# A second stream of early forward transforms in a two-layer image kernel

## The chip, the cores and the metric

The kernel runs on one core of a Trainium2 chip. A core has five engines that each work through their own instruction list in order: PE (TensorE, matrix products into PSUM), ACT (ScalarE, activation functions and copies), DVE (VectorE), POOL (GpSimd) and SP (SyncE, which issues nearly all DMAs here). They meet only through semaphores. The metric is the time of one execution on the device in microseconds (us), smaller being better.

## The reference

Everything is float32. The input `x` has the shape (4, 128, 128, 128): four batch entries, 128 channels, images of 128x128. Two layers follow one another.

The first layer takes the 16384 pixels of a batch entry as one sequence of tokens. Each token passes a small MLP, a projection to two halves of 256, a causal convolution of four taps, and then a state space scan with 256 channels and 16 states:

```
h = h * dA + d_t * B_t * u_t          # per channel and state, along the 16384 tokens
y = sum over states of h * C_t
out = (y + u * D) * silu(z) @ out_proj_w.T
x1 = silu(group_norm(out)) + x
```

The second layer works on whole images of `x1`. It transforms, multiplies with four learned filters that are mixed by four weights, and transforms back:

```
weights = softmax(mean(relu(agg_w @ group_norm(x1))) @ wg_w.T + wg_b)   # 4 weights per batch entry
xf      = rfft2(x1)
out     = irfft2(xf * xf * sum_f weights[f] * filt_f) + 0.5 * x1
```

(The reference transforms back and forth between the filter and the product; the kernel uses that this changes little more than single columns of the spectrum, and multiplies directly.) The mixture weights of a batch entry need the whole of its `x1`, but the forward transform `rfft2` of an image needs only that image.

## The kernel before, in words

There are two Python functions, `block0` and `block1`, that emit one after the other the instructions of the two layers. In both the order on every engine is written out by hand (a manual schedule); the tile framework adds semaphores and buffer waits.

**`block0`.** The tokens of each batch entry are cut into 32 chunks of 512, so there are 128 chunks `k`. A chunk has 32 scans of 128 partitions by 512 tokens, in 16 *slots* (`NP = 16`) of two scans each. The list `todo[slot, phase]` holds closures, and the loop at the end of `block0` walks over absolute slots `16*k + s`, and within a slot over the phases `turn, sums, pe, exps, late, act, pool, dbu, early, gate, scans, dve, end`. What a closure emits takes that place in the list of whatever engines it uses. The parts that matter here:

- `exps` (L393, ACT) makes the decay factors `da` for the scans of the next slots, `scans` (L412, DVE) does two scans per slot and, for half of them, the product with `C` (L414). The tiles `da1`, `da2` and `da3` have one buffer each, so ACT can't run far ahead of DVE.
- `dbu_turn` (L383, PE) turns the input term of one scan in two slots into PSUM; `sums` (L433, PE) adds up states into `y`.
- `pre(k)` computes chunk `k`'s inputs during chunk `k-1`: `cv_mm(0)` and `cv_mm(1)` (L234, PE) stand in slots 0 and 1, `silu_act` (L239) and `z_silu` (L242) in slot 2, `xd_mm` (L247) in slot 3, transposes `pt_dut` (L293) in slots 8 and 11 with their ACT copies `bt` (L304) up to slot 14. `turn_bank` is a single PSUM buffer (tag `pt`) that `xd_mm`, the transposes and a few others share; `psum` hands out two buffers (tag `pp`).
- `finish` turns the raw output of a batch entry `b` into `x1` while the next entry is being scanned. In the first 18 chunks of an entry it normalises the previous one (`norm_act` L633 on ACT in slot 2, `norm_dve` L637 and `norm_stats` L641 on DVE in slot 3, two pieces per chunk); I call these *norm chunks*. From chunk 18 on it runs the aggregation (`agg`), one piece per chunk, the last four of them in the `pt` bank at slot 15.
- `spectrum(b, c0, n)` computes the forward transform of `n` images of batch entry `b` early, in `block0`, and stores it in DRAM (`spec_b`). A *unit* is eight channels of one batch entry; it is done as three sub-units of 3, 3 and 2 images, one sub-unit per chunk. Its five steps have fixed slots: `load` (4, SP), `over_h` (12, PE), `evict` (12 end, ACT copy `fs`), `over_w` (13, PE), `store` (13 end, ACT copy `fq` and a DMA). It takes both matmul results in `pp`. Batch entries 0 and 1 are eligible (`EARLY = 2`). From chunk 52 to chunk 126 this makes 25 units: all 16 of entry 0, and channels 0 to 71 of entry 1.

**`block1`.** The second layer is 64 units in the list `units`. A unit takes three *steps* (3, 3, 2 images); step `t` belongs to unit `t // 3`. Each step emits `over_h` (L851, PE), `evict`, `residual`, `conjugates` (L860, DVE), `products` (DVE), `over_w` (L874, L875, PE), `back_h` (L913, L914, PE), `back_w` (L925, PE), and each unit four scaled filters `term` (L822, ACT), three `mix` additions (L828, POOL) and two `sums` (L899, L900, POOL). For an early unit `over_h`, `conjugates` and the matmuls of `over_w` are left out; its spectrum `sx` is loaded (L815) instead. The units of entry 3 come late, because entry 3 must first be normalised and aggregated, which `finish` does in the first 36 units. `load(n + 1)` is emitted at step 0 of unit `n`, behind the filter loads `load_filter` (L805, four DMAs of 520 KB for a group of eight channels, `KEEP = 4` buffers). All of them are on SP's queue.

Of the kernel before, what the change touches and what calls it, by code (L numbers as in the profile page):

```python
# [26 lines left out]
F32 = mybir.dt.float32  # L27
# [6 lines left out]
P = 128  # L34
T = 512
DG = 32
SQ = 4
NP = 16
CC = 8
EARLY = 2  # L40
KEEP = 4
LAG = 7
EPS = 1e-5
# [3 lines left out]
def kernel(ctx: ExitStack, tc: tile.TileContext, a: dict, out: bass.AP):  # L47
    nc = tc.nc
    x = a["x"]
    B, C, H, W = x.shape  # L50
    L = H * W
    NCH = L // T
# [9 lines left out]
    WF = W // 2 + 1  # L62
# [3 lines left out]
    dpool = ctx.enter_context(tc.tile_pool(name="dram", bufs=1, space=DRAM))  # L66
# [79 lines left out]
    xflat = x.rearrange("b c h w -> b c (h w)")  # L146

    stats, outs, spectra = {}, {}, set()
    spec = [dpool.tile([H, C, 2, WF], F32, tag=f"spec_{b}", name=f"spec_{b}") for b in range(EARLY)]
    shared = SimpleNamespace(**{k: v for k, v in locals().items() if k not in ("ctx", "tc")})  # L150
    block0(tc, shared)
    block1(tc, shared)
# [2 lines left out]
def block0(tc, s):  # L155
    nc, B, NCH, NH, NS, NG, ND, R, NX, KC, HALO, C, L, NF, DI = (
        s.nc, s.B, s.NCH, s.NH, s.NS, s.NG, s.ND, s.R, s.NX, s.KC, s.HALO, s.C, s.L, s.NF, s.DI,
    )
    NT = T // P
    with ExitStack() as ctx:  # L160
        def pool(name, bufs, **kw):
            return ctx.enter_context(tc.tile_pool(name=name, bufs=bufs, **kw))
# [7 lines left out]
        psp = pool("psp", 2, space=PSUM)  # L170
        psy = pool("psy", 1, space=PSUM)
        pst = pool("pst", 1, space=PSUM)
        psd = pool("psd", 1, space=PSUM)

        def psum(n):
            return psp.tile([P, T], F32, tag="pp", name=f"pp_{n}")

        def turn_bank(n):
            return pst.tile([P, T], F32, tag="pt", name=f"pt_{n}")

        st = {}
        stats, outs = s.stats, s.outs
# [282 lines left out]
                (50, "dve", done),  # L465
            ]

        def spectrum(b, c0, n):

            g = {}  # L470

            def load():
                g["x"] = p1.tile([s.H, 3, s.W], F32, tag="fx", name=f"fx_{b}_{c0}")
                nc.sync.dma_start(out=g["x"][:, 0:n], in_=s.x1[b][c0 : c0 + n].rearrange("c h w -> h c w"))

            def over_h():
                g["pa"] = psp.tile([s.W, 3, 2 * s.WF], F32, tag="pp", name=f"pp_fa_{b}_{c0}")
                for q in range(n):
                    nc.tensor.matmul(g["pa"][:, q], g["x"][:, q], s.fh, start=True, stop=True)

            def evict():
                g["sa"] = p1.tile([s.W, 3, 2 * s.WF], F32, tag="fs", name=f"fs_{b}_{c0}")
                nc.scalar.copy(g["sa"][:, 0:n], g["pa"][:, 0:n])

            def over_w():
                half = s.H // 2
                g["px"] = psp.tile([s.H, 3, 2 * s.WF], F32, tag="pp", name=f"pp_fx_{b}_{c0}")
                for q in range(n):
                    re, im = g["sa"][:, q, 0 : s.WF], g["sa"][:, q, s.WF :]
                    for (data, a, b_), start in (((re, s.fwr, s.fwr), True), ((im, s.fwi, s.fwm), False)):  # L490
                        for at, w in ((0, a), (1, b_)):
                            o = g["px"][at * half : (at + 1) * half, q]
                            nc.tensor.matmul(o, data[:, at : at + half], w, start=start, stop=not start)

            def store():
                x = p1.tile([s.H, 3, 2, s.WF], F32, tag="fq", name=f"fq_{b}_{c0}")
                nc.scalar.copy(x[:, 0:n].rearrange("h c r k -> h c (r k)"), g["px"][:, 0:n])  # L497
                nc.sync.dma_start(out=s.spec[b][:, c0 : c0 + n], in_=x[:, 0:n])

            return [  # L500
                (4, "pe", load), (12, "pe", over_h), (12, "end", evict), (13, "pe", over_w), (13, "end", store),
            ]

        n_chunks = B * NCH
        todo = defaultdict(list)
# [19 lines left out]
        for b in range(B - 1):  # L525
            for at, phase, f in finish(s, io, b, NP + 7, norm, agg):
                todo[at + (b + 1) * NCH * NP, phase].append(f)
        chunk = NCH + NCH // 2 + 4
        for b in range(EARLY):
            for c0 in range(0, C, CC):  # L530
                chunk = max(chunk, (b + 1) * NCH + NCH // 2 + 4)
                if chunk + 3 > n_chunks:
                    break
                for at, n in ((0, 3), (3, 3), (6, 2)):
                    for slot, phase, f in spectrum(b, c0 + at, n):
                        todo[slot + chunk * NP, phase].append(f)
                    chunk += 1
                s.spectra.add((c0, b))
        for n in range(n_chunks * NP):
            if n % 2 == 0:  # L540
                todo[n - 3, "early"].append(partial(exps, n, (0,)))
# [7 lines left out]
        slots = [n for n, _ in todo]  # L549
# [172 lines left out]
def block1(tc, s):  # L722
# [7 lines left out]
    nc, B, C, H, W, WF, NF, NCH = s.nc, s.B, s.C, s.H, s.W, s.WF, s.NF, s.NCH  # L730
    HH = H // 2
    filt = s.a["filt_w"].rearrange("f c h w q -> h f c (w q)")
    with ExitStack() as ctx:
        def pool(name, bufs, **kw):
            return ctx.enter_context(tc.tile_pool(name=name, bufs=bufs, **kw))

        late = pool("late", 1)
# [30 lines left out]
        todo = defaultdict(list)  # L768
# [8 lines left out]
        rest = groups[len(wait) :]  # L777
        kept, late = wait[-KEEP + 1 :], wait[: -KEEP + 1]
        units = [(c0, b) for c0 in wait for b in (0, 2, 1)] + [(c0, B - 1) for c0 in kept]
        for n, c0 in enumerate(rest):  # L780
            units += [(c0, b) for b in (0, 2, 1, 3)]
            for c1 in late[n * len(late) // len(rest) : (n + 1) * len(late) // len(rest)]:
                units.append((c1, B - 1))
        N = len(units)
        u = [SimpleNamespace() for _ in units]

        spans = []
        for n, (c0, b) in enumerate(units):
            ft = next((x for x in spans if x.c0 == c0 and (n - x.last == 1 or (c0 in kept and b == B - 1))), None)
            if ft is None:  # L790
                ft = SimpleNamespace(c0=c0, first=n)
                spans.append(ft)
            ft.last = n
            u[n].ft = ft
        loads = defaultdict(list)
        for k, ft in enumerate(spans):
            at = max(ft.first - 4, min(k, 1))
            if k >= KEEP:
                at = max(at, spans[k - KEEP].last)
# [7 lines left out]
        def load(n):  # L807
            if n < N:
                c0, b = units[n]
                u[n].xt = p2.tile([H, CC, W], F32, tag="xt1", name=f"xt1_{n}", bufs=6)  # L810
                nc.sync.dma_start(out=u[n].xt, in_=s.x1[b][c0 : c0 + CC].rearrange("c h w -> h c w"))
                u[n].early = units[n] in s.spectra
                if u[n].early:
                    u[n].sx = p2.tile([H, CC, 2, WF], F32, tag="sx", name=f"sx_{n}", bufs=2)
                    nc.sync.dma_start(out=u[n].sx, in_=s.spec[b][:, c0 : c0 + CC])  # L815

        def term(n, f):

            if 0 <= n < N:
                tag, bufs = ("term", 3) if f else ("wb", 2)  # L820
                t = p2.tile([H, CC, 2 * WF], F32, tag=tag, name=f"{tag}_{n}_{f}", bufs=bufs)
                nc.scalar.activation(t, u[n].ft.t[:, f], AF.Copy, scale=s.wts[units[n][1]][0:H, f : f + 1])  # L822
                u[n].terms = [t] if f == 0 else u[n].terms + [t]

        def mix(n, f):
            if 0 <= n < N:
                wb = u[n].terms[0]
                nc.gpsimd.tensor_tensor(wb, wb, u[n].terms[f], ALU.add)  # L828
# [107 lines left out]

        with tc.manual_schedule():
            load(0)
            for t in range(3 * N + LAG + 3):
                n, i = divmod(t, 3)  # L940
                if i == 0:
                    for ft in loads[n]:
                        load_filter(ft)
                    load(n + 1)
                over_h(t)
                if t == 0:
                    for f in range(NF):
                        term(0, f)
                        if f:
                            mix(0, f)  # L950
                evict(t - LAG - 1)
                residual(t - LAG - 2)
                conjugates(t)
                products(t - 2)
                for f in todo[t, "add"]:
                    f()
                over_w(t - 1)
                back_h(t - LAG)
                back_w(t - LAG - 1)
                if i == 0:  # L960
                    if n:
                        term(n, 3)
                        mix(n, 2)
                    copies(n - 2)
                elif i == 1:
                    term(n + 1, 0)
                    term(n + 1, 1)
                    if n:
                        mix(n, 3)
                else:  # L970
                    term(n + 1, 2)
                    sums(n - 1)
                    mix(n + 1, 1)
                for phase in ("pe", "act", "dve", "end"):
                    for f in todo[t, phase]:
                        f()
# [79 lines left out]
```

## Time and profile before

| what | value |
|---|---|
| median of 3 runs | 7170.91 us (7170.88 to 7171.45) |
| the profiled execution's own time | 7175.45 us |
| its span | 7173.6 us |
| first scan of the first chunk, last chunk's last part | 48.7 us, about 6404 us |
| first and last store of the output | 6466.8 us, 7169.5 us |
| chunk without any finishing work (chunks 20 to 22) | 48.37 / 49.12 us in turn |
| norm chunk (40 to 42; 104 to 106) | 50.3 us |
| PE, DVE, ACT, POOL busy share of the span | 82%, 96%, 86%, 96% |
| TensorE clock granted, mean | 0.897 |

The profile comes from one execution. An engine's row counts the time in which it executes, not the time in which it issues DMAs or waits. In rows of a timeline the first number is the start in microseconds from the span's start and the second is the duration; a bracket behind it gives the idle time before, and what ended it. `L412` is line 412 of the kernel. A name such as `da<-rdelta,amat` says which tile an instruction writes and which it reads. Rows of matmuls count each float32 product as two instructions.

### The profile page before, as it was taken

How to read it: one execution, taken by the hardware profiler on the slowest of the kernel's cores; microseconds unless marked ns; L12 is line 12 of the kernel's file. 1: busy time of each engine (PE TensorE's matmuls, PEld its weight loads, DVE VectorE, ACT ScalarE, POOL GpSimd, SP SyncE). 2: the span in 40 equal slices, each digit the busy share in tenths (PEclk: the TensorE clock that was granted, in tenths of full speed). 3: DMA queues.
4: the chain of work that ended last, by engine and by line, in shares of the span. 5: the costliest groups of instructions: out<-in, count | busy, mean ns of one | idle time of the engine just before them, and what ended most of it. 6: DMA issues, size and time to landing. Idle time of an engine off the chain costs nothing.

```text
span 7173.6 us, 91384 instructions
## 1 busy us (share of the span) xinstructions
PE 5904.2 (82%) x26708; PEld 2626.8 (37%) x26708; DVE 6892.9 (96%) x7966; ACT 6143.9 (86%) x13658; POOL 6892.5 (96%) x3188
## 2 busy tenths in 40 slices
PE   6888888788787788888888788888887888867998
PEld 2333333233222233333333333333333333326888
DVE  6999999999999999999999999999999999989777
ACT  6888888888888888888888888898888888878876
POOL 6999999999999999999999999999999999988887
PEclk8888888888888889998989899999898899979999
DMA  5666666666777777777777777777777777769866
GB/s 139 160 160 152 163 159 151 165 159 165 191 176 192 179 171 176 172 184 175 189 196 186 188 176 175 178 177 184 189 191 194 177 179 177 172 164 306 236 185 162
DMA packets 905480, 1286.20 MB, mean 179 GB/s; under 512 B 81672, under 2 KB 356752, under 8 KB 904976
## 3 DMA queue, kind: packets, MB, share of 16 engines
q1 hardware_dynamic: 904832, 1280.09, 71.9%
q8 instruction: 210, 3.44, 0.2%
q14 instruction: 294, 2.41, 0.1%
q10 hardware_dynamic: 144, 0.26, 0.0%
HBM read 1023.45 MB, written 256.58 MB: 178 GB/s over the span
## 4 chain that ended last, share of the span: by engine, by line
DVE 41%; ACT 29%; issue 11%; PE 10%; DMA 5%; POOL 3%; SPq 1%; DVEq 0%; ACTq 0%; POOLq 0%
DVE da L412 20%; DVE h L412 12%; ACT da L393 12%; DVE hb L414 5%; ACT L393 3%; DMA rdelta<-dd 2%; ACT L275 2%; ACT delta L275 2%; ACT bt L304 2%; POOL hb L363 2%; DVE zs L443 1%; PE y L433 1%; POOL hb L419 1%; ACT L242 1%; DMA xt<-x 1%
## 5 line engine op out<-in xcount | busy, mean ns | idle before, releaser
L363 POOL TENSOR_TENSOR hb<-rdu,rB 128x1536 f32<-128x1536 f32 (+2 forms) x1536 | 3605.7, 2364 | 22.4 <-DMA rdelta<-dd 21.3
L393 ACT ACTIVATE da<-rdelta,amat 128x512 f32<-128x512 f32 x4096 | 2794.1, 700 | 138.3 <-DVE h L412 133.9
L419 POOL TENSOR_TENSOR hb<-h,rC 128x1024 f32<-128x1024 f32 (+1 forms) x1072 | 2435.0, 2274 | 88.8 <-DVE h L412 73.4
L412 DVE TENSOR_TENSOR_SCAN da<-da,st,hb 128x512 f32<-128x512 f32 x1976 | 2419.8, 1267 | 21.5 <-ACT da L393 14.3
L433 PE MATMUL y<-hb,sel 128*32 128x512 f32 x8192 | 1313.4, 717 | 2.9 <-POOL hb L419 2.7
L414 DVE TENSOR_TENSOR hb<-da,rC 128x512 f32<-128x512 f32 x2040 | 1296.1, 674 | 3.0
L412 DVE TENSOR_TENSOR_SCAN h<-da,st,b 128x512 f32<-128x512 f32 x992 | 1258.3, 1268 | 1.7 <-PE b L383 1.6
L412 DVE TENSOR_TENSOR_SCAN h<-da,st,hb 128x512 f32<-128x512 f32 x1000 | 1251.6, 1255 | 1.8 <-ACT da L393 1.8
L383 PE MATMUL b<-ident,bt 128*128 128x128 f32 x4096 | 748.4, 305 | 516.1 <-DVE h L412 390.6
L234 PE MATMUL pp_cv<-xm,wck 128*128 128x512 f32 x2048 | 1014.3, 640 | 1.6 <-ACT xm L217 0.8
L304 ACT ACTIVATE bt<-pt_dut,xdt 128x256 f32<-128x256 f32 x2048 | 839.4, 474 | 184.5 <-PE pt_dut L293 184.3
L383 PEld LDWEIGHTS b<-ident,bt 128*128 128x128 f32 x4096 | 531.3, 154 | 1017.1 <-DVE h L412 692.8
L415 ACT COPY st<-da 128x1 f32<-128x1 f32 x2040 | 273.1, 160 | 474.2 <-DVE hb L414 471.1
L234 PEld LDWEIGHTS pp_cv<-xm,wck 128*128 128x128 f32 x2048 | 395.9, 204 | 651.0 <-issue 422.1
L828 POOL TENSOR_TENSOR wb<-wb,term 128x1040 f32<-128x1040 f32 x192 | 461.0, 2401 | 70.8 <-ACT term L822 62.9
L293 PE MATMUL pt_dut<-ident,du 128*128 128x128 f32 x1024 | 232.4, 338 | 285.1 <-ACT xdt L286 174.9
L429 PE MATMUL y<-u,diag 128*128 128x512 f32 x512 | 303.0, 675 | 188.7 <-DVE zs L443 187.3
L293 PEld LDWEIGHTS pt_dut<-ident,du 128*128 128x128 f32 x1024 | 132.2, 162 | 604.8 <-POOL du L312 475.9
L393 ACT ACT_TABLE_LOAD x262 | 336.1, 1283 | 12.1 <-DMA rdelta<-dd 7.4
L312 POOL TENSOR_TENSOR du<-delta,u 128x512 f32<-128x512 f32 x256 | 318.8, 1267 | 25.8 <-ACT delta L275 25.8
L223 PE MATMUL pp_z<-xm,win 128*128 128x512 f32 x512 | 274.5, 634 | 51.8 <-ACT fq L497 46.2
L267 PE MATMUL pp_dt<-xd,wdt 8*128 8x512 f32 x512 | 284.8, 642 | 33.0 <-ACT pp_o L457 23.5
(160 smaller groups left out, 8139.8 us busy)
## 6 DMA issues: line engine op xcount, KB each, us to landing
rdelta<-dd SPq DMA_DIRECT2D x1024, 256.0 KB, 4.7
rdu<-dd SPq DMA_DIRECT2D x1024, 256.0 KB, 7.5
rC<-bc SPq DMA_DIRECT2D x512, 256.0 KB, 7.3
rB<-bc SPq DMA_DIRECT2D x512, 192.0 KB, 4.7
dd<-delta SPq DMA_DIRECT2D x256, 256.0 KB, 7.2
dd<-du SPq DMA_DIRECT2D x256, 256.0 KB, 5.7
ft<-in_filt_w SPq DMA_DIRECT2D x104, 520.0 KB, 7.0
ob<-o SPq DMA_DIRECT2D x128, 256.0 KB, 2.1
```

The lines of the kernel that those rows point to most:

```text
L234: nc.tensor.matmul(ps["cv", j], w, d["xm"][:, t : t + T], start=t == 0, stop=t == KC - 1)
L293: nc.tensor.transpose(ps["dut"][:, 2 * t + j, :], d["du"][:, j, at : at + P], s.ident)
L304: nc.scalar.activation(d["bt"][:, 2 * h + t, :, q, :], src, AF.Copy, scale=d["xdt"][:, 2 * h + t, R + q : R + q + 1])
L312: nc.gpsimd.tensor_tensor(du, d["delta"][:, j, :], d["u"][:, j, :], ALU.mult)
L363: nc.gpsimd.tensor_tensor(hb[:, p : p + n, :], d["du", j][:, m : m + n, :], d["B"][:, p - 1 : p - 1 + n, :], ALU.mult)
L383: nc.tensor.transpose(b[:, t * P : (t + 1) * P], src, s.ident)
L393: nc.scalar.activation(da, d["delta", j][:, m, :], AF.Exp, scale=s.amat[:, c : c + 1])
L412: nc.vector.tensor_tensor_scan(o, das[q], b, init, ALU.mult, ALU.add)
L414: nc.vector.tensor_tensor(hb[:, p + q, :], das[q], d["C"][:, p + q, :], ALU.mult)
L419: nc.gpsimd.tensor_tensor(hb[:, ps, :], h[:, q, :], d["C"][:, ps, :], ALU.mult)
L433: nc.tensor.matmul(y[m * DG : (m + 1) * DG, :], s.sel, d["hb", j, r][:, p, :], start=False, stop=r == NG - 1)
L828: nc.gpsimd.tensor_tensor(wb, wb, u[n].terms[f], ALU.add)
```

## The change

In `block0` a second stream of early units is added. The two streams are called `ways`: the old one with its slots and the `pp` buffers, and a new one with the slots `load` 13 (SP), `over_h` 15 (PE), `evict` 16 (ACT), `over_w` 17 (PE, which is slot 1 of the next chunk) and `store` 17 end, with the `pt` bank as its home. Entries 0, 1 and 2 are eligible now, and within an entry the last channels come first. Each turn gives the next unit to the way that is free first; the new way takes no entry 0, and leaves out the last four chunks of an entry. The result is 35 early units: all 16 of entry 0, all 16 of entry 1, and the last three of entry 2. The old way runs in chunks 52 to 123 and the new one in chunks 84 to 91 and 96 to 120 (33 sub-units).

In `block1` the last part of the list `units` is put in another order, so that early units and whole ones alternate; the rule that joins units to one load of filters allows one unit between them (`n - x.last <= 2`); and each image load is emitted two units ahead, at the second step of a unit, in place of one unit ahead at its first step.

```diff
-EARLY = 2
-    spec = [dpool.tile([H, C, 2, WF], F32, ...) for b in range(EARLY)]
+    spec = [dpool.tile([H, C, 2, WF], F32, ...) for b in range(B - 1)]
...
-        def spectrum(b, c0, n):
+        def spectrum(b, c0, n, slots, home):
...
-                g["pa"] = psp.tile([s.W, 3, 2 * s.WF], F32, tag="pp", name=f"pp_fa_{b}_{c0}")
+                g["pa"] = home(f"fa_{b}_{c0}", [s.W, 3, 2 * s.WF])
...
-                g["px"] = psp.tile([s.H, 3, 2 * s.WF], F32, tag="pp", name=f"pp_fx_{b}_{c0}")
+                g["px"] = home(f"fx_{b}_{c0}", [s.H, 3, 2 * s.WF])
...
-            return [
-                (4, "pe", load), (12, "pe", over_h), (12, "end", evict), (13, "pe", over_w), (13, "end", store),
-            ]
+            return list(zip(*zip(*slots), (load, over_h, evict, over_w, store)))
...
-        chunk = NCH + NCH // 2 + 4
-        for b in range(EARLY):
-            for c0 in range(0, C, CC):
-                chunk = max(chunk, (b + 1) * NCH + NCH // 2 + 4)
-                if chunk + 3 > n_chunks:
-                    break
-                for at, n in ((0, 3), (3, 3), (6, 2)):
-                    for slot, phase, f in spectrum(b, c0 + at, n):
-                        todo[slot + chunk * NP, phase].append(f)
+        ways = [
+            (((4, "pe"), (12, "pe"), (12, "end"), (13, "pe"), (13, "end")), psum),
+            (((13, "pe"), (15, "pe"), (16, "act"), (17, "pe"), (17, "end")), turn_bank),
+        ]
+        ready = [(b + 1) * NCH + NCH // 2 + 4 for b in range(B - 1)]
+        images = [(b, c0) for b in range(B - 1) for c0 in reversed(range(0, C, CC))]
+        queues = [images, [x for x in images if x[0]]]
+        free = [ready[0], ready[1]]
+        while True:
+            way = min((0, 1), key=lambda w: free[w])
+            group = next((x for x in queues[way] if x[::-1] not in s.spectra), None)
+            if group is None:
+                break
+            b, c0 = group
+            chunk = max(free[way], ready[b])
+            if chunk + 3 + 5 * way > n_chunks:
+                break
+            for at, n in ((0, 3), (3, 3), (6, 2)):
+                while way and chunk % NCH in range(NCH - 4, NCH):
                     chunk += 1
-                s.spectra.add((c0, b))
+                for slot, phase, f in spectrum(b, c0 + at, n, *ways[way]):
+                    todo[slot + chunk * NP, phase].append(f)
+                chunk += 1
+            free[way] = chunk
+            s.spectra.add((c0, b))
...
-            units += [(c0, b) for b in (0, 2, 1, 3)]
-            for c1 in late[n * len(late) // len(rest) : (n + 1) * len(late) // len(rest)]:
-                units.append((c1, B - 1))
+            full = [(c1, B - 1) for c1 in late[n * len(late) // len(rest) : (n + 1) * len(late) // len(rest)] + [c0]]
+            for b in (0, 2, 1):
+                units += [(c0, b)] + full[:1]
+                full = full[1:]
+            units += full
...
-            ft = next((x for x in spans if x.c0 == c0 and (n - x.last == 1 or (c0 in kept and b == B - 1))), None)
+            ft = next((x for x in spans if x.c0 == c0 and (n - x.last <= 2 or (c0 in kept and b == B - 1))), None)
...
             load(0)
+            load(1)
...
-                    load(n + 1)
...
                 elif i == 1:
+                    load(n + 2)
                     term(n + 1, 0)
```

On the engines' lists the new stream puts these in chunk `k`, slots 15 to 17: on PE `over_h` behind the `sums` of slot 15 and ahead of `cv_mm(0)`, and `over_w` behind `cv_mm(1)`; on ACT the copy `fs` behind the two `da` of slot 16, and the copy `fq` behind the last state copies (L415) of slot 17 and ahead of the two `da` for slot 19; on SP the image load behind the loads of slot 13 and ahead of the old stream's `spec` store, and the new `spec` store ahead of the next `xt` load.

The units 0 to 41 keep their order; of them 29, 32, 35 and 38 become early. The units 42 to 63 were `E F F F F F F` three times and one `F` more (E for early, F for whole); they become `E F E F E F F`, `E F E F E F F`, `E F E F E F F F`.

More of the change, by code (lines that the diff above doesn't have):

```diff
@@ L148 @@
     stats, outs, spectra = {}, {}, set()
-    spec = [dpool.tile([H, C, 2, WF], F32, tag=f"spec_{b}", name=f"spec_{b}") for b in range(EARLY)]
+    spec = [dpool.tile([H, C, 2, WF], F32, tag=f"spec_{b}", name=f"spec_{b}") for b in range(B - 1)]
     shared = SimpleNamespace(**{k: v for k, v in locals().items() if k not in ("ctx", "tc")})
@@ L173, in block0, with psum, turn_bank @@
         psd = pool("psd", 1, space=PSUM)
[L175 to L179, printed above, removed]
+        def psum(n, shape=(P, T)):
+            return psp.tile(list(shape), F32, tag="pp", name=f"pp_{n}")
+        def turn_bank(n, shape=(P, T)):
+            return pst.tile(list(shape), F32, tag="pt", name=f"pt_{n}")
         st = {}
```

## The prediction

> **What bounds the kernel now.** I read the page first, then the busy times of stretches, then the order in time of three engines at the place where the second stream lands, last the waits and the chain of the second block.
>
> ```profile
> span 7173.6 us, 91384 instructions
> PE 5904.2 (82%) x26708; PEld 2626.8 (37%) x26708; DVE 6892.9 (96%) x7966; ACT 6143.9 (86%) x13658; POOL 6892.5 (96%) x3188
> ```
>
> The first block ends near 6404 us, so 89% of the span is there. The next view is busy time by stretch (start:end, length, busy of PE, PEld, DVE, ACT, POOL, granted clock, DMA share, GB/s): one chunk of the first block, then three stretches of the second.
>
> ```profile
> 5216.00:5267.00 51.00, 41.55 (x185) 16.65 (x184) 50.97 (x56) 44.15 (x100) 50.83 (x25) 0.90 0.77 191
> 6470.00:6661.00 191.00, 142.29 (x1086) 134.18 (x1087) 172.18 (x384) 154.47 (x301) 162.90 (x85) 0.95 1.00 308
> 6661.00:6890.00 229.00, 215.73 (x1683) 196.83 (x1683) 173.91 (x419) 198.59 (x429) 202.87 (x106) 0.99 0.71 203
> 6890.00:7151.00 261.00, 233.95 (x1968) 231.32 (x1967) 190.40 (x454) 189.82 (x387) 213.19 (x110) 0.95 0.72 190
> ```
>
> In the chunk DVE has 0.03 us of idle time in 51. Whatever makes it wait is added to the span; ACT, with 7 us idle, must deliver each `da` in time. The last stretch, units 39 to 60, is PE's, with gaps that the chain and the waits name:
>
> ```profile
> by line: DMA xt<-x 16.9%; PE po L925 14.1%; PE pz L913 13.8%; PE pz L914 13.7%; PE pa L851 13.7%; PE px L874 12.0%; PE px L875 11.8%; issue 0.7%; ACT term L822 0.4%; DVE ot L932 0.4%; ACT y L906 0.2%; ACT xs L876 0.2%; DVE sq L885 0.1%; ACT
> PE pa L851 <- DMA xt<-x: 23.6, 6, 5.3
> L828 POOL TENSOR_TENSOR wb<-wb,term 128x1040 f32<-128x1040 f32 x66 | 158.5, 2401 | 28.6 <-ACT term L822 26.3
> ```
>
> PE stood 23.6 us for six late images. POOL needs (158.5+28.6+28.5)/22 = 9.8 us a unit (mixes and two sums).
>
> **The second stream in the first block.** The trace holds 75 sub-units (25 units of 3); the changed one has 105: 72 in the old way, 33 in the new, at chunks 84-91 and 96-120. Today's stream is free: norm chunks last 50.30 us with it (chunk 105, from 5266.84 to 5317.13) and 50.30 without (chunk 40). That is the cheap end for the new one.
>
> But the new slots are 15, 16 and 17, and there each engine's order matters. This is order in time at chunk 104/105 (start, length, engine, line): PE, ACT, DVE. Slot 16 starts with the scan at 5266.84, slot 18 with that at 5272.73.
>
> ```profile
> 5264.32 1.06 PE L433 MATMUL y<-hb,sel 128*32 128x512 f32 x8
> 5265.32 3.70 PE L234 MATMUL pp_cv<-xm,wck 128*128 128x512 f32 x8
> 5268.86 0.60 PE L383 MATMUL b<-ident,bt 128*128 128x128 f32 x4
> 5269.39 1.06 PE L433 MATMUL y<-hb,sel 128*32 128x512 f32 x8
> 5270.39 3.70 PE L234 MATMUL pp_cv<-xm,wck 128*128 128x512 f32 x8
> 5274.05 0.66 PE L383 MATMUL b<-ident,bt 128*128 128x128 f32 x4
> ...
> 5272.90 1.31 ACT L393 ACTIVATE da<-rdelta,amat 128x512 f32<-128x512 f32 x2
> 5274.23 1.28 ACT L242 ACT_TABLE_LOAD   x1
> 5280.42 0.69 ACT L393 ACTIVATE da<-rdelta,amat 128x512 f32<-128x512 f32 x1
> ...
> 5272.73 1.27 DVE L412 TENSOR_TENSOR_SCAN h<-da,st,b 128x512 f32<-128x512 f32 x1
> 5275.67 2.46 DVE L412 TENSOR_TENSOR_SCAN da<-da,st,hb 128x512 f32<-128x512 f32 x2
> 5279.23 1.28 DVE L637 TENSOR_TENSOR of<-pp_n,xr 128x512 f32<-128x512 f32 x2
> ```
>
> PE runs without a pause from 5264.32 to 5273.93. In the changed order `over_h` stands before the first `pp_cv` and `over_w` behind the second. In the old stream they take 5256.34 to 5257.01 (0.67) and 5258.78 to 5260.26 (1.48) for three images, 0.71 an image. So `over_w` would end at 5273.93+2.13 = 5276.06, its last matmul 0.27 later. On ACT the copy `fq`, which waits for it, stands ahead of the two `da` at 5272.90, which wait for nothing today. Behind them wait the table load, `zs`, `u`, the norm's two `pp_n` and the `da` at 5280.42.
>
> ACT's delay, with v the end of the second `pp_cv` after slot 18's start: v + 0.71n + 0.27 + 0.06 (semaphore, from gaps of that size) + 0.37 (the old `fq`, 5261.11 to 5261.48; 0.26 for two images) - the `da`'s present start. That start is 0.79 after slot 18 in 31 of the 33. DVE's delay is ACT's less the smallest slack behind: 0.70 in norm chunks (second `pp_n` done at 5279.11, read at 5279.82), 0.35 in the others (chunk 116, `da` done at 5835.61, scanned at 5835.95). Read from the trace chunk by chunk:
>
> - norm, n=3, v 1.17: 1.17+2.13+0.70-0.79-0.70 = 2.51 us, 10 times: 25.1
> - norm, n=2, v 1.10: 1.62, 5 times: 8.1
> - other, n=3, v 1.47: 3.15, 10 times: 31.5
> - other, n=2, v 1.27: 2.14, 6 times: 12.8
> - chunks 97 and 113, where v is 4.43: about 6 each: 12
>
> Sum 89.5, less 1 for the old stream's chunks 124-126, which it leaves: **+88 us**. Without the slacks the sum is 108; the free old stream gives 33 times 0 to 0.28 (chunks 52-63: 49.03 on average, against 48.75 in clean ones), at most +9, or 0. I take 88, by the rows of the very place. ACT has gaps of 1.00 and 1.51 us in slots 16 and 17, so `fs` and the 0.85 us of copies themselves fit. DVE cannot pass the waiting scan, and has no slack to win it back.
>
> SP: the new image load (196 KB) stands ahead of the old `spec` store, which waits until 5261.6 for `fq` today; it waits for `over_h` at 5257 and lands, behind `of` (5261.61), by about 5263, before PE needs it at 5265.3. The new store waits until about 5277 ahead of the next `xt` load (now 5268.6); `xt` is first needed nine slots into the chunk, near 5295. Both hidden; without that cover each us late would be a us of DVE's.
>
> **The second block.** Ten units more are early: 29, 32, 35, 38 and six of 42 to 60 (three are early there now). Each drops 24 of 48 transform matmuls, three ACT copies and three DVE multiplies, and adds a 532 KB load.
>
> - Units 39 to 60: 261 us now, and 24.7 of it are gaps (22 whole units at 10.72, their steady period, are 236). A load two units ahead is issued two of a unit's three steps earlier, about 7 us, against waits of at most 5.3, so these go. With units alternating PE needs (10.7+5.35)/2 = 8.0, so POOL is next: 9.8. I take 10.2 for 19 units and 10.72 for three: 226, **-35**. Ends: 9.8 gives 218 (-43), 10.72 throughout -25.
> - Units 29 to 38: 110.4 us, 11.0 each; ACT is near 90% busy there. Four lighter units: **-4** (0 to -8).
> - 6470 to 6661: DVE busy 172 of 191 with `xt` and `sx` waits in the chain; the DMA share is 1.00, so earlier loads mostly queue. **-8** (0 to -19).
> - Start: one more image ahead of the first filter, 0.5 MB at the 300 GB/s there: **+1.5** (0 to 3).
> - Filters of groups 14 and 15 are loaded one unit ahead, not four, and 15 twice. In the trace the first of four lands 5.3 us after issue and its `wb` would run about 10 after: **+1** (0 to 4).
>
> Together -44.5, ends -70 and -18.
>
> [...] The row says 0.95 granted in 6470:6661, where two units of three are early, so PE needs 8.5 and stays below POOL. [...]
>
> **Sum.** 7173.6 span plus 1.85 around it is the profiled 7175.45, 4.5 above the runs' median of 7170.91. 7175.45+88-44.5 = 7219, which on the median's scale is 7214.
>
> **The rivals.**
> - *The stream is free* (faster): the wait at `fq` costs DVE nothing, as the old stream's does. For it: equal chunks with and without the old one, POOL as busy as DVE. Against: the old `over_w` comes where ACT is behind, the new one where ACT waits for DVE. 7171+5-44.5 = 7131. It decides below 44.5/33 = 1.35 us a sub-unit.
> - *Stall, little gain*: POOL and its mixes keep units at 10.7, and the first stretch stays with DMA: 7171+88-20 = 7239. For it: a DMA share of 1.00 and 26.3 us of POOL waiting for `term`.
> - *Wider stall*: the slacks are gone, because ACT arrives late at each following `da`, or images land late: 7171+108-44.5 = 7234.
>
> **How the numbers follow.** Chances: forecast 0.57 (7190 to 7238 by itself), free 0.20, little gain 0.15, wider 0.08. A range of 7136 to 7255 leaves out about half of the free case and the worst of the other two. Within 0.2% (14 us, about what a measurement can tell) needs a stall of 30 to 58 us: 0.06. Faster 0.19, slower 0.75.
>
> **What would show it.** Right: chunks 98-112 at 52 to 53 us in place of 50.30; a DVE wait of 1.5 to 2 us on `da`, and an ACT wait on the new `pt_fx` matmul, 33 times; units 42-60 near 10.2 us, no `xt` wait there. Wrong: norm chunks at 50.3, or filter waits on ACT at units 49 and 56 of several us, or late units at 10.7.

## The result and the profile after

The changed kernel takes 7220.05 us (median; 7218.53 to 7222.08) where the kernel before takes 7171.18 (7170.88 to 7173.31). The ratio is 1.0068 [1.005, 1.0085]: the change makes the kernel 48.9 us slower. The profiled execution has a span of 7217.0 us, 43.4 more than before.

That is two large amounts of opposite sign. In the profile before, the first scan of the last chunk's last slot pair starts at 6403.96; after, at 6513.43. So `block0` lost 109.5 us. From there to the end it takes 703.6 us in place of 769.6, so `block1` gained 66.1. The page shows almost nothing of this, because the shares of the engines hardly move:

```profile
span 7217.0 us, 92202 instructions
PE 5912.8 (82%) x27028; PEld 2618.5 (36%) x27028; DVE 6884.9 (95%) x7936; ACT 6152.9 (85%) x13688; POOL 6892.6 (96%) x3188
```

DVE is busy 8 us less and the span is 43 longer: the loss must be waiting time. Busy time by stretch (start:end, length, then PE, PEld, DVE, ACT, POOL, granted clock, DMA share, GB/s), for one norm chunk with a sub-unit of the new stream, and for the three stretches of the second block that the prediction showed of before, each as long as it is now:

```profile
5317.00:5371.00 54.00, 44.22 (x204) 17.75 (x203) 51.15 (x55) 44.81 (x101) 50.73 (x25) 0.91 0.76 189
6579.00:6770.00 191.00, 142.00 (x1116) 133.70 (x1117) 177.18 (x398) 161.27 (x317) 169.59 (x88) 0.97 1.04 322
6770.00:6979.00 209.00, 192.31 (x1459) 171.87 (x1458) 162.51 (x393) 186.28 (x402) 195.79 (x102) 0.98 0.85 241
6979.00:7194.00 215.00, 198.84 (x1679) 191.08 (x1678) 179.56 (x436) 179.43 (x369) 211.55 (x110) 1.00 0.87 235
```

In the first row DVE has 2.85 us of idle time in 54, where it had 0.03 in 51. In the last row POOL is busy 211.55 of 215 and PE no longer leads.

Order in time of PE, ACT and DVE where the new stream's `over_w` lands (start, length; line numbers in `block0` are one less than before). Slot 18 starts with the scan at 5323.19:

```profile
5321.52 3.70 PE L233 MATMUL pp_cv<-xm,wck 128*128 128x512 f32 x8
5325.15 0.44 PE L492 MATMUL pt_fx<-c_fwr,fs 128*64 128x130 f32 x4
...
5326.63 0.66 PE L382 MATMUL b<-ident,bt 128*128 128x128 f32 x4
...
5323.31 0.16 ACT L414 COPY st<-da 128x1 f32<-128x1 f32 x1 [0.44 <-DVE hb L413]
5326.75 0.49 ACT L496 COPY fq<-pt_fx 128x390 f32<-128x390 f32 x1 [3.28 <-PE pt_fx L492]
5327.13 1.31 ACT L392 ACTIVATE da<-rdelta,amat 128x512 f32<-128x512 f32 x2
...
5331.85 1.48 ACT L644 ACTIVATE pp_n<-of,bias,scale 128x512 f32<-128x512 f32 x2
...
5323.19 1.27 DVE L411 TENSOR_TENSOR_SCAN h<-da,st,b 128x512 f32<-128x512 f32 x1
...
5327.86 2.47 DVE L411 TENSOR_TENSOR_SCAN da<-da,st,hb 128x512 f32<-128x512 f32 x2 [1.64 <-ACT da L392]
...
5332.66 1.39 DVE L648 TENSOR_TENSOR of<-pp_n,xr 128x512 f32<-128x512 f32 x2 [1.16 <-ACT pp_n L644]
```

PE works without a pause, so `over_w` runs when the second `pp_cv` is done, at 5325.15. ACT reached the copy `fq` at 5323.47 and stands 3.28 us. The two `da` behind it start at 5327.13, 3.94 after slot 18, where before the change the first started 0.17 after it. DVE then loses 1.64 us on the `da` and 1.16 more on the norm's `pp_n`, which ACT also brings late. Over the whole span the waits (us in total, times, longest) say the same:

```profile
ACT fq L496 <- PE pt_fx L492: 107.5, 33, 4.8
...
DVE da L411 <- ACT da L392: 72.2, 61, 3.1
...
DVE h L411 <- ACT da L392: 25.3, 21, 1.4
```

The last two read before the change:

```profile
DVE da L412 <- ACT da L393: 14.3, 8, 2.9
DVE h L412 <- ACT da L393: 2.1, 4, 0.7
```

33 waits of ACT, one for each sub-unit of the new stream, are 107.5 us; the block lost 109.5. DVE's waits for `da` grew by 81.1 us, and 18.6 for `pp_n` are new.

In the second block the chain of the stretch from 6979 to the end, by line, and the group of the mixes there (busy, mean ns, idle before), answer to the rows of before where PE stood for late images:

```profile
by line: POOL wb L841 24.6%; issue 9.3%; DVE pr L905 7.3%; PE po L938 5.6%; POOL y L912 5.5%; POOL y L913 5.0%; PE pz L926 4.8%; PE pz L927 4.6%; ACT term L835 4.2%; DVE ot L945 4.0%; PE px L887 3.7%; PE px L888 3.6%; PE pa L864 3.3%; DVE s
...
L841 POOL TENSOR_TENSOR wb<-wb,term 128x1040 f32<-128x1040 f32 x66 | 158.8, 2406 | 3.5
```

`DMA xt<-x` is gone from the chain (16.9% before), POOL leads it, and POOL's idle time ahead of its mixes fell from 28.6 to 3.5 us. The gains by units, from one output store to another:

| part of the second block | before | after | difference | predicted (filters, +1, apart) |
|---|---|---|---|---|
| the scan at 6403.96 (6513.43) to the first output | 62.86 | 63.80 | +0.9 | +1.5 |
| units 0 to 28 | 312.11 | 299.20 | -12.9 | -8 (its first 191 us) |
| units 29 to 38 | 110.35 | 102.18 | -8.2 | -4 |
| units 39 to 60 | 261.23 | 215.28 | -45.9 | -35 |
| units 61 to 63 | 18.97 | 18.86 | -0.1 | |

### The profile page after: what moved, and what is told of

The parts are those of the page before. It is cut to its first block, busy times and chain, and to the rows that moved or that the text cites. A ratio compares the mean times of both kernels' runs of the same rounds, so it can differ in the third digit from the quotient of the medians.

```text
span 7217.0 us, 92202 instructions
## 1 busy us (share of the span) xinstructions
PE 5912.8 (82%) x27028; PEld 2618.5 (36%) x27028; DVE 6884.9 (95%) x7936; ACT 6152.9 (85%) x13688; POOL 6892.6 (96%) x3188
## 4 chain that ended last, share of the span: by engine, by line
DVE 36%; ACT 35%; PE 12%; issue 10%; DMA 3%; POOL 3%; SPq 1%; DVEq 0%; ACTq 0%; POOLq 0%
DVE da L411 16%; ACT da L392 14%; DVE h L411 10%; DVE hb L413 4%; ACT L392 4%; PE pp_cv L233 4%; ACT bt L303 3%; PE y L432 3%; DMA rdelta<-dd 2%; ACT L274 2%; ACT delta L274 2%; ACT L241 2%; ACT u L238 1%; ACT zs L241 1%; PE y L428 1%
## 5 line engine op out<-in xcount | busy, mean ns | idle before, releaser
L246 PE MATMUL pt_xd<-u,wx 128*40 128x512 f32 x512 | 259.9, 632 | 74.8 <-ACT u L238 74.8
```

## The experiments

The theory is the prediction's: ACT stands at `fq` because the copy has its place in ACT's list ahead of the `da`, while its data come late on a PE that is full until then (theory A). The rival is that the stall comes from the stream's work itself, wherever it stands: its matmuls and copies, its loads and stores, or the shared bank (B). For the second block, the gain may come from ten more early units (C), from the early loads (D) or from lighter units that alternate (E), and its next bound may be POOL (F) or a chain beside POOL (G).

### The copy one slot later

```diff
-            (((13, "pe"), (15, "pe"), (16, "act"), (17, "pe"), (17, "end")), turn_bank),
+            (((13, "pe"), (15, "pe"), (16, "act"), (17, "pe"), (18, "end")), turn_bank),
```

> The new stream's second copy (fq, on ACT) is put one slot later, from the end of slot 17 to the end of slot 18, behind the two da of slot 19, the table load, z_silu, u and the norm's pieces. All work stays. Theory A (order on ACT: the copy waits 3.3 us for over_w and holds back everything behind it): over_w is done by then, the wait is gone, norm chunks go from 53.4 and 52.5 back to 50.3 to 50.7, and of the 110 us that the first block gained 100 to 110 go: 7110 to 7122 us. Rival B (the second stream's work itself is too much for PE, ACT and the queues, wherever it stands): chunks stay at 52 to 53 us, 7200 to 7225 us.

Measured: 7115.59 us (7110.88 to 7117.89), ratio 0.9926 [0.9914, 0.9939]. All 33 sub-units are still done, on the same engines and in the same bank; one entry of a tuple separates 7220 from 7116. The copy's store moves with it. Norm chunks are back at 50.30 us; the other chunks behind a sub-unit are within 0.9 us of the kernel before, 0.1 longer on average. In order of time, ACT and then DVE and PE, with slot 18 at 5273.64:

```profile
5273.81 1.31 ACT L392 ACTIVATE da<-rdelta,amat 128x512 f32<-128x512 f32 x2
...
5278.53 1.48 ACT L644 ACTIVATE pp_n<-of,bias,scale 128x512 f32<-128x512 f32 x2
5279.94 0.48 ACT L496 COPY fq<-pt_fx 128x390 f32<-128x390 f32 x1
...
5276.58 2.46 DVE L411 TENSOR_TENSOR_SCAN da<-da,st,hb 128x512 f32<-128x512 f32 x2
...
5280.48 1.91 PE L246 MATMUL pt_xd<-u,wx 128*40 128x512 f32 x4 [0.89 <-ACT fq L496]
```

The `da` start 0.17 after slot 18 again, `fq` runs 6 us behind them without a wait, and DVE waits for neither `da` nor `pp_n`. The last row shows the price: the bank is held longer, and PE's `xd_mm` now waits for `fq`. The view of the bank's tile `pt_fx` says who waited for it (us, times):

```profile
  PEld pt_xd L246: 39.7, 28
  PE pt_xd L246: 15.0, 14
```

These waits cost at most a few us, because PE has the time there (46.74 us busy of 54 from 5317 to 5371): the block ends at 6408.30 against 6403.96 before the change. Theory A holds, and this kernel is faster than both others.

### The matmuls earlier

```diff
-            (((13, "pe"), (15, "pe"), (16, "act"), (17, "pe"), (17, "end")), turn_bank),
+            (((13, "pe"), (15, "pe"), (16, "act"), (17, "sums"), (17, "end")), turn_bank),
```

`sums` is the phase just ahead of `pe`, so `over_w` is issued ahead of the second `pp_cv`.

> ACT's order is left as in the changed kernel; on PE the new stream's over_w goes ahead of the sums and of the second cv_mm of slot 17, so that it ends about 4.5 us earlier, before ACT reaches the copy. All work stays. Theory A: no ACT wait at the copy, norm chunks at 50.3 to 50.8, 7110 to 7125 us. If u (silu) then waits for the later cv_mm, up to 1 us a chunk comes back (33 us, 7150). Rival B (the work itself): 7200 to 7225 us.

Measured: 7115.49 us (7109.93 to 7122.93), ratio 0.9928 [0.9915, 0.9942]. This is the other end of the same wait: the copy stays where the change put it, its data come earlier, and the wait is gone. The view of the tile `pt_fx` lists the idle time ahead of its instructions (us, times):

```profile
  issue: 3.4, 20
  ACT da L392: 2.2, 13
```

These 33 are PE's, ahead of the weight loads; ACT has none ahead of its 33 copies, where the changed kernel has the 107.5 us. Two edits with nothing in common but this wait recover the same 104.5 us. Rival B would have left the loss in both.

### The new stream's matmuls done twice

```diff
-                for q in range(n):
+                for q in [q for _ in range(1 + (home is turn_bank)) for q in range(n)]:
```

In `over_w`, for the new stream alone; the second time writes the same values.

> The new stream's over_w is issued twice (the second time over the same result), 1.48 us more PE work for three images and 0.98 for two, 43 us in 33 sub-units. Theory A: DVE's delay grows by the same amount, norm chunks go from 53.4 to 54.9 and from 52.5 to 53.5, in all +43 us: about 7263 us. Rival B (amount of work): PE has 18% of idle time, so 43 us of matmuls add 0 to 10 us: 7220 to 7230 us.

Measured: 7259.0 us (7255.17 and 7262.83, two runs alone), ratio 1.0127 [1.0108, 1.0145]: 39 us more than the change as it is, where theory A expected 43. Norm chunks grow by 4.43 us (three images) and 3.10 (two) against the kernel before, where the change as it is adds 3.09 and 2.21: 1.34 and 0.89 more, against the expected 1.48 and 0.98. ACT's wait grows with it (us, times, longest):

```profile
ACT fq L496 <- PE pt_fx L492: 146.0, 33, 6.1
```

ACT waits 38.5 us longer in all, and the last scan of the block starts 36.3 us later (6549.71 against 6513.43). At this place PE's work passes through ACT to DVE nearly one for one.

### The second stream left out

```diff
-        free = [ready[0], ready[1]]
+        free = [ready[0], 10 * n_chunks]
```

> The second stream is left out, the order of the channels, of the units and the loads two units ahead stay; 25 early units again (all of entry 0, groups 7 to 15 of entry 1). Theory A: the first block is as in the kernel before, within 2 us of 6404; the second block gains from loads and order alone: units 39 to 60 have 6 early ones, PE needs 16 x 10.7 + 6 x 5.35 = 203 us, POOL 211, so about 215 to 225 us there in place of 261, less some 10 us lost at units 2 to 20, of which seven become whole: 7120 to 7140 us. Rival C (the second block's gain comes from ten more early units): 7155 to 7175 us.

Measured: 7130.43 us (7129.13 to 7131.06), ratio 0.9947 [0.9934, 0.9961]. Rival C (7155 to 7175) falls: units 39 to 60 take 221.27 us with six early units among them, against 215.28 with nine and 261.23 before. So the change to `block1` is worth 38 us without the new stream, and the stream itself is worth 14.8 us more when it does not stall (7130.43 against 7115.59 of the first experiment, on one chip). As the change puts it in, the kernel is 89.6 us slower with it than without (7220.05 against 7130.43, medians).

### Loads two units ahead, alone and taken back

The kernel before with this one part of the change:

```diff
             load(0)
+            load(1)
...
-                    load(n + 1)
...
                 elif i == 1:
+                    load(n + 2)
```

> The kernel before with one part of the change alone: image loads two units ahead. Theory D (the loads carry a large part of the second block's gain): the first 28 units gain the 13 us that they gained in the changed kernel, where the early units among them are the same; units 39 to 60 lose their 24.7 us of waiting for xt and stay with PE at 10.7 us a unit, 236 to 238 us; together -35 to -40: 7128 to 7135 us. Theory E (the gain is that of lighter, alternating units; loads matter little): 7155 to 7170 us.

Measured: 7132.43 us (7128.41 to 7133.59), ratio 0.9946 [0.9931, 0.9961]; units 39 to 60 take 227.90 us (-33.3), units 0 to 28 301.28 (-10.8), units 29 to 38 107.55 (-2.8). The gain in the late units is more than the 24.7 us of gaps that were there to be closed. Busy time of those units (columns as above) shows where the rest is from:

```profile
6879.00:7107.00 228.00, 223.44 (x1971) 221.24 (x1970) 187.39 (x453) 188.91 (x388) 213.72 (x111) 1.00 0.80 215
```

PE does the work that took it 233.95 us before (1968 instructions in 261 us, in the prediction's last row) in 223.44, and the granted clock is 1.00 in place of 0.95. The late images cost twice: PE stood for them, and its matmuls were slower too, by 10.5 us in all (the clock is taken up again below).

The same lines taken out of the changed kernel:

> The changed kernel with the image loads put back to one unit ahead, emitted behind the filter loads. Theory D: the first 28 units go back to about 312 us (+13), and units 39 to 60 get waits for xt again, some 10 to 20 us of the 46 that they gained, as there are seven filter loads with an image load behind them: 7240 to 7255 us. Theory E: 7218 to 7228 us.

Measured: 7251.04 us (7249.94 to 7259.51), ratio 1.0115 [1.01, 1.013]. Units 39 to 60 take 233.87 us (+18.6 against the change), units 0 to 28 309.39 (+10.2), units 29 to 38 109.68 (+7.5). The waits for images that the change had ended are back, and now for spectra too (whole span: us, times, longest):

```profile
PE pa L864 <- DMA xt<-x: 34.4, 12, 5.5
...
ACT px L882 <- DMA sx<-spec: 10.1, 2, 5.3
```

In the changed kernel neither wait occurs. In units 39 to 60 the clock falls with them from 1.00 to 0.96:

```profile
6992.00:7226.00 234.00, 204.01 (x1684) 198.07 (x1683) 180.87 (x436) 181.09 (x370) 213.17 (x111) 0.96 0.82 220
```

So early loads carry half to two thirds of the second block's gain (theory D): from the last scans of `block0` to the end, 43.8 us when added and 34.2 when taken back, of 66.1.

### The old order of units

The changed kernel with the two old lines that build the last part of `units`:

```diff
+            units += [(c0, b) for b in (0, 2, 1, 3)]
+            for c1 in late[n * len(late) // len(rest) : (n + 1) * len(late) // len(rest)]:
+                units.append((c1, B - 1))
```

> The changed kernel with the units of the last part in the old order (three early ones together, then four whole ones), 35 early units and loads two ahead kept. If alternation is what lets POOL (9.6 us a unit) be the bound in place of PE: early units run at 9.6, whole ones at 10.7, so units 39 to 60 take 9 x 9.6 + 13 x 10.7 = 226 us in place of 215: about 7230 us. If the buffers between the engines even this out: 7218 to 7223 us.

Measured: 7231.57 us (7229.85 to 7232.49), ratio 1.0085 [1.007, 1.01]. Units 39 to 60 take 225.29 us against 215.28 with units alternating. The order is worth 10 to 12 us in this kernel: the later ones of whole units that follow one another take 10.72 us each again, where whole and early ones in turn take 9.70 and 9.43. Waits for images are back too (8.1 us of PE's, four times), so the run does not tell the order's own worth from that of the loads which it brings too close together.

### One mix of every second late unit moved to DVE

The first experiment's kernel, in `mix`:

```diff
-                nc.gpsimd.tensor_tensor(wb, wb, u[n].terms[f], ALU.add)
+                (nc.vector if f == 1 and n > 28 and n % 2 else nc.gpsimd).tensor_tensor(wb, wb, u[n].terms[f], ALU.add)
```

> The kernel with the copy one slot later, and from unit 29 on the first of the three mix additions of every second unit on DVE in place of POOL. If POOL is the bound of the late units (98% busy there), taking 2.4 us from it every second unit gives 0.4 to 1.2 us a unit: units 39 to 60 in 190 to 207 us in place of 215, about 7095 to 7108 us. If PE or the chain of waits is the bound: 7113 to 7122 us.

Measured: 7124.9 us (7122.41 to 7131.13), ratio 0.994 [0.9923, 0.9956]. A miss of both expectations: 9 us slower than without the edit. Units 39 to 60 take 222.64 us in place of 215.16, although POOL has much less to do (columns as above; then waits):

```profile
6876.00:7100.00 224.00, 201.18 (x1695) 192.71 (x1694) 194.37 (x452) 180.41 (x372) 188.31 (x100) 1.00 0.83 225
```

```profile
PE po L938 <- DVE ot L945: 13.3, 14, 1.2
POOL wb L841 <- DVE wb L841: 12.7, 4, 3.4
```

POOL is at 188.31 of 224, and waits for DVE's part of its own sum; PE waits 13.3 us for DVE's `ot`, 2.5 without the edit. The run says that the move is no gain, not yet whether POOL was the bound, since DVE's new work may have cost what POOL's relief gave.

### The same mix left out

The first experiment's kernel again; in those units the sum lacks one of its four filters.

```diff
+                if f == 1 and n > 28 and n % 2:
+                    return
```

> The kernel with the copy one slot later, without the first of the three mix additions of every second unit from unit 29 on: that filter's part is missing from those units, and the output is not the reference's there. Nothing is put on DVE for it. Theory F (POOL is the bound of units 39 to 60, and the run with the addition on DVE lost the gain to DVE's own work): 195 to 207 us there in place of 215, about 7097 to 7108 us. Theory G (a chain through DVE, ACT and PE sets 9.7 us a unit beside POOL): 212 to 216 us there, 7112 to 7118 us.

Measured: 7113.45 us (7110.39 to 7119.41), ratio 0.992 [0.9904, 0.9937], the same as with the mix. Units 39 to 60 take 214.84 us against 215.16. Busy time of the stretch, and then the chain from 6900 to 7060 by line:

```profile
6873.00:7088.00 215.00, 200.06 (x1684) 191.93 (x1683) 179.84 (x436) 179.69 (x370) 187.59 (x100) 1.00 0.87 235
```

```profile
by line: DVE pr L907 21.2%; ACT term L835 16.2%; ACT wb L835 8.8%; DVE sq L901 8.5%; DVE ot L947 8.5%; issue 8.3%; DVE sa L875 7.8%; DVE sq L900 6.3%; DMA ft<-in_filt_w 3.6%; ACT sa L868 3.1%; DVE sz L934 2.9%; SPq L818 2.2%; ACT px L886 1.
```

and ACT's largest wait in the stretch (us, times, longest):

```profile
ACT wb L835 <- DVE pr L907: 25.2, 22, 1.2
```

POOL has 27 us to spare in 215 and nothing moves. The steady pair of an early and a whole unit takes 9.44 and 9.71 us between its stores, as it does with the mix (9.43 and 9.70). So POOL at 98% was not what alone set the period (theory G against F), although the chain of waits ran through it. What does set it stays open. The chain now alternates between DVE's products `pr` and ACT's `term` and `wb`. ACT waits for `pr` each time it makes a new `wb`; that tile has two buffers, so the wait is for the unit before the last one. Whether this loop is the bound, a third buffer would tell; no run has one. PE is now the busiest engine, at 200.06 of 215.

## Why the prediction was right, and where it was not

The forecast was 7214, slower, with a range of 7136 to 7255; measured 7220.05. The sign and the mechanism held. The closeness of the number is partly luck: the loss was sized 21 us too small and the gain 22 us too small.

**The stall, +88 predicted, +109.5 measured.** The place, the engine that waits and the queue behind it were as described (first and second experiment), and so was the growth with `over_w` (the doubled one). The step that failed is the present start of the `da` in the formula for ACT's delay, "0.79 after slot 18 in 31 of the 33". That is the start of the second of the two `da`. The row that the prediction itself quoted, at 5272.90 for both of them (x2), has the first 0.17 after the scan at 5272.73, and `fq` pushes that one. The error is 0.62 us, 31 times: 19.2, and 88 + 19.2 = 107.2. By kind of chunk (growth of a chunk against the same one before, mean):

| chunks with a new sub-unit | predicted | with 0.17 for 0.79 | measured |
|---|---|---|---|
| norm, 3 images (10) | 2.51 | 3.13 | 3.09 |
| norm, 2 images (5) | 1.62 | 2.24 | 2.21 |
| other, 3 images (10) | 3.15 | 3.77 | 3.79 |
| other, 2 images (6) | 2.14 | 2.76 | 3.07 |
| 97 and 113, the two together | 12 | | 8.5 |

So the slacks, 0.70 and 0.35, and the durations were well sized; one start was read from the wrong instruction of a group. The two chunks read one by one, 97 and 113, were sized 3.5 too large.

**The second block, -44.5 predicted, -66.1 measured.** Late units: -35 predicted, -45.9 measured, beyond the end of -43. The step "I take 10.2 for 19 units and 10.72 for three" stood midway between POOL's 9.8 and PE's 10.72. All 22 units came out at 215.28 / 22 = 9.79 on average, which was the lower end, and those at 39 to 41, taken at 10.72, too (9.70, 9.44, 9.70). The reason given for 9.8 was POOL, and the last experiment takes that away as the sole reason: the number held and its cause did not. The other end, 10.72 throughout, rested on all the work of PE outside the gaps staying as long as it was; with the loads alone it became 10.5 us shorter, at a granted clock of 1.00 in place of 0.95. Units 29 to 38: "four lighter units: -4"; measured -8.2. The loads alone gain 2.8 there and the lighter units alone, with the loads taken back, 0.7; what was missing is that the two gain together, and the loads had no term. The first stretch: "-8 (0 to -19)". Up to the store of unit 17 (193.7 us behind the first one before, 185.3 now) the gain is 8.4, as predicted, 6.7 to 8.6 of it from the loads; the DMA share is 1.04 there now, at 322 GB/s in place of 308. Units 18 to 28 gain 4.5 more and had no term.

**The start and the filters.** +1.5 predicted, +0.9 measured; with the same early loads the other runs have +1.0 to +5.2 there, so this term is not settled. The feared ACT waits for filters of several us at units 49 and 56 do not occur: ACT's waits for `ft` after the start are three, of at most 0.9 us.

**SP.** As predicted: the new image load is issued at 5307.66 and lands at 5312.08, 3.7 us before PE needs it, and the new store is issued at 5327.26 ahead of an `xt` load that lands at 5330.54, long before its use.

**The clock.** The prediction took the 0.95 of its row 6470:6661 for the late units, and so put PE at 8.5 us a unit there. The granted clock in the late stretch is 1.00 after the change, where it was 0.95 before. What PE waits for in that stretch, after the change (us, times, longest), is never long:

```profile
PE pz L926 <- ACT y L919: 9.7, 9, 1.1
PE po L938 <- DVE ot L945: 3.1, 5, 1.3
```

With loads one unit ahead the same list begins with

```profile
PE pa L864 <- DMA xt<-x: 17.7, 5, 5.4
```

and there the clock is 0.96; so it is 0.95 before the change, with waits up to 5.3, and 0.96 with the old order of units, with waits up to 3.7. The trace of before shows the link pause by pause. In the stretch from 6889 to 7151 its clock records hold 1.00 and 0.50 alone, with six periods at 0.50, five of 3.41 us and one of 6.83, 23.9 us in all. Each begins within 1.4 us of the end of one of PE's six pauses (neither a product nor a weight load) of 3.12 to 5.23 us; no other pause there is longer than 1.07. In the first of the periods (6905.10 to 6908.50) PE worked without a pause and did 18 instructions in 3.40 us; at 1.00, from 6910 to 6936, it did 232 in 26. With the old order of units a pause of 2.15 us had such a period behind it (a row of PE with the pause in its bracket, then busy times as above):

```profile
7067.78 0.49 PE L924 MATMUL pz<-c_ihc,y 128*128 128x128 f32 x2 [2.15 <-ACT y L917]
7069.20:7072.50 3.30, 3.30 (x18) 3.30 (x18) 2.53 (x6) 3.30 (x6) 3.30 (x3) 0.50 0.96 310
```

Shorter pauses did not always bring one: after the change, from 6579 to 6770, PE has five pauses of 2.29 us, three with a period at 0.50 behind them and two (up to 6636.64 and 6736.06) without. From 6979 to 7194 the longest pause is then 1.31 us, and nothing in that stretch is at 0.50. So the clock spoke for the change: it ends the long pauses, and with the loads alone, at a clock of 1.00 as well, PE's work was 10.5 us shorter. I had no term for this.

**The rivals.** The free stream (7131) fell: it decides below 1.35 us a sub-unit, and the measured loss is 109.5 / 33 = 3.3. It is what the first two experiments made of the kernel, and better than its price, since the second block gains more. Little gain (7239) fell with the -66.1. The wider stall named the right sum, 108, for a reason that did not hold: its slacks are still there.

## What to carry to other kernels

A copy out of PSUM can cost its engine the time until the matmul is done (here 3.28 us in one sub-unit) and not only its own 0.49 us, and everything behind it in that engine's list pays; where a short step is put in a full schedule, first write down when its input is ready and when the next instruction behind it must start, then move the copy behind that one or its producer ahead. When a duration or start is taken from a row that joins several instructions (x2), ask which of them the new wait will push. And take a change of several parts apart before giving it up: here 7220 was a 7116 with one entry of a schedule in the wrong slot.

## What the runs showed of the hardware

- An engine that was busy 98% of a stretch, and led its chain of waits, did not by itself set its length: with 24 us less work for POOL in 215, units 39 to 60 changed from 215.16 to 214.84 us.
- The same addition moved to DVE, at 194.37 busy of 224, cost 7.5 us in those units, though DVE had been idle 16% of the time (179.44 busy of 215).
- In the late stretch TensorE's granted clock fell at single pauses of PE: before the change it stood at 0.50 for 3.41 or 6.83 us at each of the six pauses of 3.12 to 5.23 us and at 1.00 in the rest of the stretch; after it, with pauses of up to 1.31 us, at 1.00 throughout. Of five pauses of 2.29 us earlier in the second block, after the change, three had a period at 0.50 behind them.
- The mean clock of a stretch did not follow PE's busy share: before the change it was 0.95 both at 142.29 busy of 191 and at 233.95 of 261, with loads one unit ahead in the changed kernel 0.96 at 204.01 of 234, and 1.00 at 198.84 of 215 after the change. With the loads alone it is 1.00 at 223.44 of 228: at nearly the same count of instructions as before the change (1971 and 1968), PE was busy 10.5 us less in 22 units.
